# Sums over scan states and gathered rows by adding DMA transfers, a convolution as three products on TensorE, and new orders for the five queues

## The chip, the cores and the metric

The kernel runs on one core of one Trainium2 chip. A core has five engines that are programmed each with its own list of instructions: TensorE (PE) for matrix products, VectorE (DVE), ScalarE (ACT) and GpSimd (POOL) for element-wise work, and SyncE (SP), which here only issues DMA transfers. POOL also issues transfers, the indirect ones among them. Each engine takes its instructions strictly in the order of its list and waits at an instruction until what that needs is there. On chip there are two memories: SBUF (128 partitions), which all engines and the DMA engines reach, and PSUM, into which PE writes and from which DVE and ACT read. Everything else lies in DRAM.

The metric is the device time of one execution in microseconds, lower is better.

## The reference, cut to what matters

Eight sequences of 1024 tokens with 128 channels go through two layers. Each layer has two parts, and each part adds its result to `x`:

```python
x = x + L0_attn(layernorm(x))   # linear attention with a decaying state
x = x + L0_ffn(layernorm(x))    # 8 experts of width 352, two of them per token
x = x + L1_attn(layernorm(x))   # convolution over 3 tokens, then a selective scan
x = x + L1_ffn(layernorm(x))    # 8 experts of width 128, two per token, and 2 shared ones
```

The change touches `L1_attn` and the ends of the two expert parts. Of the third part:

```python
x = u @ Win + b_in
x = xp[:, :-2] * w[:, 0] + xp[:, 1:-1] * w[:, 1] + xp[:, 2:] * w[:, 2] + b   # xp: x with a zero token at both ends
x = silu(x)
dt = softplus(x @ Wdt + bdt); Bm = x @ Wb + bb; Cm = x @ Wc + bc
dA = exp(dt[..., None] * A)                                # 16 states per channel
dBx = dt[..., None] * Bm[:, :, None, :] * x[..., None]
h = dA_t * h + dBx_t                                       # token by token
y = einsum('bdn,bn->bd', h, C_t)                           # the sum over the 16 states
return y * silu(u @ Wg + bg) @ Wout + bout
```

In an expert part the result of a token is the sum over its two chosen experts, each weighted.

## The kernel before, in words

**Tiling.** A sequence's `x` stays in SBUF as 128 partitions by 1024 columns (8 chunks of 128 tokens). The attention parts work with channels in the partitions and the 1024 tokens along the columns, so that one DVE scan instruction runs over all tokens of one state.

**Order of the work.** The program writes every step as an operation with an engine, an estimated time, and the buffers that it reads and writes (`op`, and helpers such as `tt`, `stt`, `act`, `mm_cols`, `load`). The generators `l0_attn`, `l0_ffn`, `l1_attn` and `l1_ffn` of several sequences are advanced in turn by a table of times (`TIMES`); that gives the operations and their dependencies. In which order each engine then takes them is written out by hand in `ORDER`: one string per engine (PE, DVE, ACT, POOL, SP) that names for each place the sequence and how many of its waiting operations are skipped. `Schedule.run` walks through these five strings with the estimated times, gives each buffer a place in its group (four `st`, one `y`, four `tmp`, and so on), and emits the instructions. The estimates decide which of the free places a buffer gets, not the order itself. Several sequences are in work at once; the parts of different sequences are interleaved on each engine.

**The scan (`state`, L1251).** For each of 16 states ACT computes `da` = exp(dt * A), PE spreads B over the partitions into a PSUM tile `wide`, DVE multiplies it by `dtx` (in L561), DVE scans (L1262) into one of four `st` tiles, PE spreads C, and DVE multiplies `st` by it. The product of state 0 goes straight into the tile `y`; for each later state POOL adds `st` to `y` (L561, on POOL). There is a single `y` tile, so the scans of the sequences follow one another on it. Seven sequences work on all 1024 tokens at once; the last one takes its tokens in two halves, so its tiles have 512 columns.

**The head of `l1_attn`.** PE multiplies by `win` into PSUM (L610). ACT copies the result with its bias into a padded tile `xp`, ACT forms the first tap into `xs`, DVE adds the other two taps with two `scalar_tensor_tensor` (L567), and ACT applies silu.

**The expert parts.** `dispatch` normalises, routes, and scatters the token rows into a DRAM table `xd` ordered by expert, with 16 indirect transfers from POOL (L1029) that read `xw` and a copy of it in `tmp` (L1008). Blocks of 128 rows are then read back (`xg`), multiplied with the weights of their expert (`we` or `fe`, fetched by SP), weighted and written to a DRAM table `yd`. `combine` (L1041) gathers the rows of the first choice with 8 indirect transfers (L1048) into a `tmp` tile and adds the tile to `x` on POOL (L561), then does the same for the second choice. At most three such transfers are on their way at once (`ONWAY`).

**The first layer's scan.** `l0_attn` loads for each of 8 features a tile `kv` (512 KB, from `v_rows` in DRAM), multiplies it by `kT` (L561), scans it with `lam` (L935) and multiplies it by `qT` (L561), all on DVE, with all inputs in SBUF.

Of the kernel before, what the change touches and what calls it, by code (L numbers as in the profile page):

```python
# [11 lines left out]
F32 = mybir.dt.float32  # L12
# [6 lines left out]
P = 128  # L19
T = 1024  # L20
# [29 lines left out]

PE, DVE, ACT, POOL, SP = ENGINES = "PE", "DVE", "ACT", "POOL", "SP"
HOP = 0.1
TABLE = 1.3
ONWAY = 3


FREE = "wide", "acc", "row", "tile64", "xg", "xgT", "h", "ysb"
# [19 lines left out]
        0a0a0a0c0b0a0a1a1a1a1c0a1a0a1a0a0b0a0a0a1a0a1a1a1a2a1a1a2a2a2b2a2a0e0a1a0a0a0f0a0a0a1a0b0a2a  # L77
        0a0d0a0a0f0a1a0b0a0g0a0a0a0a2a0b0a0a0d0a2a0b0a0e0a3a0a0a3a0f0c3a3c0a0a0a0a3a0b3a0a0c0a0a0a0d
        0a2a0b0a0a0d0a2a0a3a0a0a0a2a1a3a0a1a1c1a1f1a1a1a3a1a1k1a1e3a1b1a1a1a3a1b1a1g3a1b1a1a1a1b1a1b
        1a1a1a1a1b1a1h1c1a1a1a1h1a1b1a0a1a0a0a2a1b2a0a0a1a2a1a1a0a1a0b1c0c0a0a1g1a0b1a0a1b1a0a0a1a1b  # L80
        0a0a1a1a0d0b0a0d1a0c0a0b2a0a2d0a2h2a2a0a2a2a2a0a0a2b2a0a2e2a0a2a2b2a0a0a2e2b2a2a0b0a2c2a2a2c
        0a2g0a2b2a0a2i2a2a2a2a0a0a2b2a2a1a2a2e1a2b1a0a2b2a0a1a1a2a0b0b2b0b0a0a2a2a0a1a2a1a0a1a2a2b2a
        2a1a2b1a2a1b2a2a1a3a2a3a1a2b2a2a2a3a1a0a1d0a1a0c0a0a1a0c0a1c2a0a1a1e0a0b0a1a0c1a0a1a0b1c0a1a
        0a4a0a1a4b0a4c0b0a0d4a0c0a1b0a1b4a1b1a4a0b0a1c1a1a0c1a0a0a1b0a0b1a0a3a3a3a0a0b0a1a0a3a3a3b3d
        3a3a2a3f3a3a3h3a2a3b3a2a3a3a3b3a4a1a3a2a2a3a4a1a3a3a3a4a3a3a3a3b3f3b3i2b3a2a2a3a3b5a3a5a5a5b
        3c5a3b5a1a3a1a3a1b1b3a3d3a3g3a1a3a2b1a3b3a1a3a1a2c3a3e2a1a3a2c3a4a3b2a3a3a2b2b2a3a2b2c3a4a4a
        1c1a2a1b1a2a1d2a1a4a2a1a2a1a2a1a1b2b1a2a2b1a1b1a2a4a2a1a1b2a1a5a1a1b4a2b1b1d1a2c2a1b1a2c1c1b
        2a1a2a1b1a2a1a1c1b1a5a1b1a3a1a3a3a4a4a4h4c4a4a4i4a4a5a4a4a5a4b3a4a4a4a3a2a4b4a4a2a4a4a4a4a4c
        4a4a3a4a3a5a4a2a3a4c4a2a3a2b2c4a4b2b2a4a2a4a5a2b4a3a4a2a4a4a3a4a3a4a3a4a4b4a3a4c4a3a4a5a3a4b
        4a4a3b5a3a4a2a4a2a4a4a3a4a2c3a5a4a2a3a4a2a4a2a3a2a2a3a3a3b2c4a4a3a2a2a2a3b2a3a2a2c3b2a3c3a2a  # L90
        3e2a2a3a2a6a3b2d2c6a3a2a6a2b3b3a2a6a2a6a2a6a2b3a2a3a2d2c2a2a6a2a2a2a5a5b5a5b5f5b5a6a4a5a4a4a
        5a3a6a3a4a3d4a5a3a3a5b3a3a5b5a3a3a4a5b5a4a5a4a5a4a5h5a5a4a4b4a5a5b5a5a5b5a7a5a4a7a4a5a5b5a7a
        5a3a7a3b3a3a3a7a5a5a7a5a3c5c3a5a3a5a3c5a4a5b5a5b3a5a5c3a5b5a3c5a5a4a5a5b5a6a5a4a5a3a5a3a5a7a
        5a5b5a3a3b5a3a6a4a6a4a3a3a3a3a4a3c3b7a4a3a4a6a3c3a4b4a6a3a4a3b4a3b3a6a3a4b3a4a4b7a3a3a4b4b4c
        4b3a4a5a4a5a4a5a3a5a4a6e6a5a7a6b6a6b6a5a6a5c6c7a5b6b6f6a7a6a6a6a4a4a6a5a6a6a6c6b6a5a6e6a6a5a
        4a6b6a4a4b6a6d6b6a4b4a5a6a4a6a6d4a6a5b6a5a6a4b5b6a6a4a6a6b6a5a6a5a6a7a6a5b6b6a5a6b6a7a6a5a6a
        4a6a4a6a7a4c6b6a5a6a5a5a4a5b6a4a4a5a6a4b4a5a5b6a5c4c6a5a4c4a5a4a5b4a5c4a4d4a4b5a5b5a4a5b5a4a
        4a4a4b7a7a7a4a7a7a7a4a7a7b7a4a5a7c4d7a4a7a7a4a5a4a7a4a7c4a4a7a4c7a7a7a7c4a7a4a6a7a7a4a7a7c7a
        6a7a6a7a7b7a7e7i7b7a5a7a7a7a6a6a7c7a5a7a5c5b7a7a7a5c5b5a7b7b7e7b6a7a5a5a7b7a7a6a7d7a7a6a6a7c
        7b6a7a6a7a6b6a6c6a6a5a5b5a5a6b5a5a5b6c6a6b5b5a6a6a5a5a5c6c6a5a6a5b5a6a5a5a6a5d6c5c6a5a6a5a5a  # L100
        5a7a5a6b5b6a5b5a7a6a5b5a7a5a5b7a6a5a6a7a6b5a5a6a5a5a7a7b7c7c7b7b7c7b7a6a6a7b7a7a6a7a6a7a6b6b
        6b6a7a7d6a7b7a7c7d7a6a7c7c7a7j7b7b7a6a7b7a7a7a7d7a7c7c6a7c6b6a6a7c7b7b6a6c6a7b7a7a6b7a6a7a6a
        7c7b7a6a7d6c7a7a6a6b7a6a7b7b6c7d6a7b7a6a6c7e6b7a7a7a6a7b7a7a6a7c7a6b6c7b7a6a7a7a6a7b6a7b6b6a
        6d6c6a7a6a6a6a6a7z7b7a7a7a7a7a7a7a7a7b7a7a7a7a7a7b7b7c7c7a7a7b7b7a7b7e7b7a7a7b7c7a7b7a7b7g7b
        7c7a7b7c7a7a7b7b7a7b7b7c7a7a7a7b7b7a7a
    """,
    DVE: """
        0a0e0a0a0a0a1a0a1e1a1bwawa0a0a0a0a0a0a0a0a1a1a0a1a0b0d0b0a0a0a0a0a0a0a0a0a0b0a0a0a1b1a1a1a0b
        1d0a1d1e0a0e0a0b0a0a1a1c0a2a1a1b1c1a0a0a2e0a0a0a0a0a0a0a0a0a0a0a0d0d0s0a0a0a0a0a0m0a0a0a0a0d
        1b0a0c2b0c0c0c0a1a2a2a2a1b1a1a1b1a2a1a1b1b0a1a1a1a1a1a1b1d1a1a1a3a1a3e3a3b3a2b2a2a0a3a2a0a2a  # L110
        2a0a2a1a1a2d2a1a2a0a1a1a1a2a1a1a1a0a1a1a1a1a1d1d1a1a1a1a1a0a1m1a1a1a1a1a3a1h1a1b1b1b1b1b2a0a
        2a0a2d2a0a2c2c2a0a1a2a2a0a2c0a2c2a0b0a0a0a2a2a3a3a0a3a0a3b3b0a3c3b3b0a3a3b0a3a2a3a0a3a3a3a3b
        0a3b3b3a2a1a3a1a3a3a1a3a3a3a1a1a1a3a1a3a1a1a1a1a1a0a2a2a2a2a2b2a1a0b0a0a0b0a2a0a1a1a1a0a0a0a
        0a2a2a1b1a2a2a2a2a2a2a2a2a2a2a2e2e2t2s2a2a2a0a2a2a2a0d2a2a2a2a2a2c2c2c0a2a0a0b2a0a0a0a0b2a2a
        1a0b0a0a0a0a1a0b0a0a1a0a0a0a1a1a0a0a0a0b0a0c0a0b0c0a0b0b0b0a0a0a2a2a0a0a2a0a0a0a2a0a2a0a0a2a
        0a0a0a2a2a0b0b0a2a0a0a0a0a2a1a2a1e1a1a1a1a0a2a1a0a0a0a0a0a0a0a3a0a2a4a2a3b3a3a3a0a3a1b1b3a1b
        4b4a2a4a4a0a0a1a0a0a0a0a2a0a0a0a0a0a0a0a0a0a0a0a1a0c1d0c0c4a0a1a0b1a0a0a0a0a0a0i0a0a0b0b0b0a
        0a0b0a0a0a1a1a2a2a0a1a1a0a1a1a1a2a1a2a1a1a4a2a1a1a1a2a3a3a1a3a3a3a3a3a3a3a3a3a3a3a3a3c3c3a3q
        3a3o3a3a2a3a3a3a3a3a3a3a3a3a3a3a3a1g0a1a1a1a0a1a1a1b1a0a1b1b0a1f1a1a1a1a1b1a0a1b1a1a0a0a1b1b
        1b1b0a1a4a1a0a1a1a1a1a1a0a1c1a4a1a0a1a2a2a2d0a3a2b2a1a2a3a4a2a4b4b4a3a2a4e3a4b4a3a4c2a4a4b3a  # L120
        4b3a4b1a2a2a3a4b1a4a3a4a4a4b4a4a2a1a2d2a4b2a3a2a2a4b5a3a5b1a5d5a5a5a1a1a1a3a3a5a2a2a2a1b1a2a
        2a1a4a3a4a5b5a5c5a3a3a1a1a5b1a1a1a1a1a1a1a5a1a1a1a1z1a1a1a1a1a1e1a1b1b1b3a1a1m1a1a1a1a3a1d1d
        2b1d1f1d1d2b1a1a1a5b3a1a5b1a2c2c3a5b1a3a2a2c2c5a2a3a3a2b2a2a2a4a4a4a2b2b4e4a4b4a4a1b2a1a4a2b
        2a2a2a2a2a2a1a2a2a2b1a2b2c2c1a2b4a4a2a2a4a4a4a4a4a2a4a4a4a4a4a1a4e4a4a4a4b4a4a4a4m4m4a4a4a4a
        4a4a4b4b4a4a4a4a2a1a2b2a2a2b1a2b2c5a5a1a2c5b2a2a1a3a3a3b3a3a5a3a5c3a1a5c1a5g2a5g5a5b4a3a5b4a
        3a5a5a4a3a5b5a3a4a4a2a4a2a3a4a4a2a2a3a3c3a3a4a2a2b2a2a3a4a2a2a3a3a5a3a3a3a4a2a4a2a3a2a2a2a2a
        2a2a2a2a2a2a2a2a2a2a2a2e2e2c2a2a2b2b2b2b2a2j2j2a2c2c2a2b2b2c2b4a2b2a5a5a5b4a2b3a3a2a5a5a5a3a
        4a4a3a3a5a3a3a5a4a3a6a4a3a3a3a4a4a3b6b6a6a6a5a5a3a6a5a5a5a5a5a5a5a5a5a5a5a5a5a5b5a5a5p5o5a2a
        5a4a3a3a3a5a4a5a5a5a5d5d5d5d5a5c5a3a5a3a2a3a3a4a2a3a3a3c3a3a3a6a3b2a3a2a3a3b3d3a3a3b2a2a3a3b
        3b3c3a3b3b3a2b2a6a3a6a6a6b3a6a2a3a6a6a6a2a6a2a6a6a6a4a4b4d4a4a4a3a5a4a6a5a3a3d3a3a3a6a6c6a3a  # L130
        5a4b6a6a6a4b4b5a4a3a3a3a3a3a3a3a3a3a3a3a3a3a3a3a3a3a3a3a3c3a3b4a3a3a3a3a4d4a4a3a3a3i4a3h4a3h
        3c3a3b3b3d3b3a5b3a7a3a7b7d7a7a5a3a4a7a4a7a4a4a5a4a4a5a4a4a4b4a4a5a5a5a4a5a4a5a3a6a6c6a7a5a3a
        6b7d7a7e3a7a5a7a5a4a5a3a6b7a5a4a5a6a7b4a5a7b4a7a5a7a7a5a3a7a7a7a5a4a7a7a3a6a4a7a6a4a6a6e6b3a
        4b6a6a6a7b6a4a4a4a4a3a4a7a3a4b4a6a6a4a6a6a4a6a6a6a6a6a4a6a6a6a6a6d6d6a6r6a6a6a6a6m3a6a6a6a6a
        6d6d6a6c6a6a6a6a4a4b4a4a7a4b5a4b3a4b5a5d5a5a5a4b5a4b4b4a4a4a4a5b7a4a5b5b3a7a7a7a4a4a5b5a5d5a
        5a5b6a5a6a6a5a5a7a5b5b4a6a7a6a4a4a6a5b4a4a6a4a4a4b4a7a5a4a7a5a6a7a5a6a7a5a4a4a6a7a4a4a4a4a4a
        4a4a4a4a4a4a4a4a4a4a4e4a4d6a4b4q4c4c4c4c4f4a4i4e4a6a4d4f4a4c4c5a6a4a4a5a4a5b5b6a5a4b7a7a5b6a
        4a5b6a5a6a6a5a5a5a6a5a7a7a6a5a7a7a7a7a7a7a7a7a7a7a7a7a7c7a7b7a7a7a7m4a7m7a6a7a7a7a7d7a7c7c7c
        7c5a5a5a6a5a7a7a5a5a4a5a6a5a5a5a4a5b5b5c5a5b5c4a5a4a5b5c5a5b5a4a5a4a5a5a5a7a4a7a7a5a7a4a5a7b
        7a5a4a4a6a5a6e5a7a5b5a5a7a6b6a6a5a6a6a6a5a7a4a7a7a7a6a7a6a6a7a7a6a6d5a5a6a6a7a6a6a5J5a5a5a5a  # L140
        5a7a5a5a5a5a5a5a7a5a5a5a5a5a5d5d5b5a5a5a5a5l5a5j5a5a5a5a5a5a5a5a5a5a7a6a5a6a5a7a6a7a6a7a6a6a
        6a7a6a6a6a6a6e6a6a6a6b6a5a5a6b6b6c6c6c6a6a5a6a5a6a6a6a6a6a5a6a5a6a6a7a7e7b7a7a7a6a7a6a5a6a6a
        5a6a6a7a6a5a7a6a7a7a5a6b6a6a7a6a5a7a5a7a6a6a7b6a7a7a7d7a7a7b7c7c7b7b7e7b7b6a7b6a6a6a6a6d6a6a
        6a7a6a7c7a7b7a7a7a7a6a6a7a6a6a6a6a6a6a6a6a6a6a6a6a6a6a6a6c6a6a6b6o6b6o6b6b6b6b6e6e6e6e6e6b7a
        6a6d7a7e7b7a6c7a7b6a7c7e7a7b7c6a7d6a7d7a7b7b7b7a7a7a7a7a7b6a7f7a7a7d7e7a7d7e7e7a7c7c6a6a7c7c
        7c7c7a7a7L7a7O7a7a7I7I7a7a7G7G6a7a7a7b6a7a7a7e7a7a7a7b7c7a7b7b6a7e7a6a7a7a7g7b7m7a7a7a7a7b7a
# [1342 lines left out]
```

## Time and profile before

| | |
|---|---|
| median of the runs (two) | 1825.53 us (1820.12 and 1830.94) |
| profiled execution | 1821.74 us |
| its span, first to last instruction | 1820.0 us |
| mean granted TensorE clock | 0.859 |
| ACT table loads | 171, 219.4 us |
| DMA | 283.59 MB, mean 156 GB/s |

| window, us | PE busy | DVE busy | ACT busy | POOL busy | DMA share |
|---|---|---|---|---|---|
| 0 to 120 | 63.7 | 79.0 | 39.6 | 3.6 | 0.94 |
| 120 to 300 | 153.8 | 120.1 | 73.6 | 68.7 | 0.71 |
| 300 to 600 | 226.5 | 242.2 | 193.6 | 161.6 | 0.51 |
| 600 to 900 | 235.8 | 261.4 | 183.2 | 160.4 | 0.55 |
| 900 to 1200 | 239.7 | 251.6 | 170.0 | 160.8 | 0.58 |
| 1200 to 1500 | 229.2 | 228.4 | 178.9 | 179.9 | 0.54 |
| 1500 to 1640 | 84.1 | 121.2 | 87.0 | 94.4 | 0.35 |
| 1640 to 1740 | 71.0 | 86.8 | 48.6 | 54.2 | 0.28 |
| 1740 to 1820 | 62.7 | 40.2 | 21.6 | 20.0 | 0.30 |

The profile is of one execution. A row of its groups names the line, the engine and the operation, then the tile written and the tiles read, the shape, and the number of instructions; behind the bar stand the busy microseconds of them all and the mean nanoseconds of one; behind the next bar the idle time of the engine just before them and what ended most of it. L561 and L610 are lines of helpers (`tt` and `mm_cols`), so there the tiles tell which step it is. The answers for one tile give the minimum, median and maximum of an instruction in place of the mean. The "chain" is the sequence of steps that ended last, followed back from the end; its shares say where the time to the end went. In the chain in order of time each piece has its start and its length in microseconds; a DMA piece runs from the issue to the landing. Of a DMA queue the page gives the packets, the megabytes and the share of the time of all 16 DMA engines that the packets took.

The scans of the second layer run on the tile `y` from 360 us (sequence 0) to 1733 us (sequence 7).

### The profile page before, as it was taken

How to read it: one execution, taken by the hardware profiler on the slowest of the kernel's cores; microseconds unless marked ns; L12 is line 12 of the kernel's file. 1: busy time of each engine (PE TensorE's matmuls, PEld its weight loads, DVE VectorE, ACT ScalarE, POOL GpSimd, SP SyncE). 2: the span in 40 equal slices, each digit the busy share in tenths (PEclk: the TensorE clock that was granted, in tenths of full speed). 3: DMA queues.
4: the chain of work that ended last, by engine and by line, in shares of the span. 5: the costliest groups of instructions: out<-in, count | busy, mean ns of one | idle time of the engine just before them, and what ended most of it. 6: DMA issues, size and time to landing. Idle time of an engine off the chain costs nothing.

```text
span 1820.0 us, 23716 instructions
## 1 busy us (share of the span) xinstructions
PE 1366.3 (75%) x7053; PEld 931.1 (51%) x7053; DVE 1430.9 (79%) x2188; ACT 996.2 (55%) x1707; POOL 903.6 (50%) x677
## 2 busy tenths in 40 slices
PE   4658898768777778768877878876887796646778
PEld 1115666446564546436664446633665765423545
DVE  4795683698896979996898886999889358888946
ACT  3325343856865575645755556356755476753632
POOL 0032504185368604876368632277457547667440
PEclk7868999789978999888988889868997998866699
DMA  8967786346455655554656447642565755312332
GB/s 185 224 150 187 216 258 196 98 139 190 139 150 165 206 150 148 140 168 154 180 148 199 130 123 232 194 120 79 175 176 172 217 174 154 105 58 63 103 103 64
DMA packets 215992, 283.59 MB, mean 156 GB/s; under 512 B 24376, under 2 KB 173368, under 8 KB 215864
## 3 DMA queue, kind: packets, MB, share of 16 engines
q1 hardware_dynamic: 200504, 250.46, 48.7%
q0 software_dynamic: 15360, 31.61, 5.7%
q8 instruction: 57, 0.93, 0.2%
q14 instruction: 71, 0.58, 0.1%
HBM read 224.73 MB, written 63.15 MB: 158 GB/s over the span
## 4 chain that ended last, share of the span: by engine, by line
DVE 44%; PE 26%; DMA 9%; ACT 9%; issue 8%; POOL 3%; another core or an unknown queue 1%; SPq 0%; DVEq 0%; ACTq 0%; POOLq 0%
DVE st L1262 10%; PE wide L610 7%; DVE wide L561 6%; PE wide L1141 5%; DVE kv L935 4%; DVE kv L561 4%; DVE st L561 4%; DMA kv<-v_rows 4%; PE wide L948 4%; DVE h L561 3%; PE acc L800 3%; DMA we<-w_rows 2%; DVE tile L561 2%; PE acc L1120 2%; DVE stats L629 2%
## 5 line engine op out<-in xcount | busy, mean ns | idle before, releaser
L1048 POOL DMA_INDIRECT tmp<-yd,at x240 | 265.3, 1106 | 197.1 <-DMA xg<-xd 82.8
L561 POOL TENSOR_TENSOR y<-y,st 128x1024 f32<-128x1024 f32 (+1 forms) x135 | 291.1, 2157 | 141.0 <-DVE st L561 116.7
L1141 PE MATMUL wide<-xgT,we 128*128 128x128 f32 x2208 | 303.0, 292 | 42.5 <-DMA we<-w_rows 14.2
L1141 PEld LDWEIGHTS wide<-xgT,we 128*128 128x128 f32 x2208 | 282.6, 205 | 73.3 <-issue 16.3
L1262 DVE TENSOR_TENSOR_SCAN st<-da,wide 128x1024 f32<-128x1024 f32 (+1 forms) x128 | 274.1, 2147 | 6.9 <-POOL y L561 2.0
L610 PE MATMUL wide<-term,eye3b 96*128 96x512 bf16 x512 | 190.3, 457 | 101.5 <-DVE st L1262 49.8
L1029 POOL DMA_INDIRECT xd<-xw,at x120 | 132.7, 1106 | 238.4 <-DVE at L786 191.8
L533 ACT ACT_TABLE_LOAD x171 | 219.4, 1283 | 3.8 <-PEq L1475 0.7
L1120 PE MATMUL acc<-we,h 128*128 128x128 f32 x1104 | 167.9, 292 | 42.1 <-DVE h L561 22.3
L1095 ACT ACTIVATE ysb<-acc,xg 128x128 f32<-128x128 f32 x345 | 116.6, 362 | 147.9 <-PE acc L1120 70.1
L1120 PEld LDWEIGHTS acc<-we,h 128*128 128x128 f32 x1104 | 149.2, 202 | 76.8 <-issue 27.8
L561 DVE TENSOR_TENSOR h<-h,wide 128x384 f32<-128x384 f32 x184 | 99.5, 545 | 106.2 <-ACT h L586 78.3
L586 ACT ACTIVATE h<-wide 128x384 f32<-128x384 f32 x184 | 89.4, 490 | 160.9 <-PE wide L1141 133.3
L561 DVE TENSOR_TENSOR wide<-dtx,wide 128x1024 f32<-128x1024 f32 (+1 forms) x144 | 158.2, 1102 | 19.2 <-PE wide L610 18.0
L586 ACT ACTIVATE da<-dt,a_mat 128x1024 f32<-128x1024 f32 (+1 forms) x144 | 149.0, 1050 | 34.8 <-DVE st L1262 28.5
L948 PE MATMUL wide<-kv,sum_e 128*32 128x512 f32 x256 | 139.8, 701 | 36.9 <-DVE kv L561 35.7
L561 DVE TENSOR_TENSOR st<-st,wide 128x1024 f32<-128x1024 f32 (+1 forms) x135 | 147.0, 1096 | 15.0 <-PE wide L610 6.9
L935 DVE TENSOR_TENSOR_SCAN kv<-lam,kv 128x1024 f32<-128x1024 f32 x64 | 150.6, 2358 | 0.7
L1029 POOL DMA_INDIRECT xd<-tmp,at x120 | 124.7, 1039 | 48.2 <-issue 35.6
L1008 POOL COPY tmp<-xw 128x1024 f32<-128x1024 f32 x15 | 16.7, 1112 | 228.8 <-ACT xw L645 172.7
L610 PEld LDWEIGHTS <-eye3b 96*128 96x128 bf16 x512 | 57.1, 112 | 141.2 <-issue 130.9
L1372 PE MATMUL acc<-xgT,fe 128*128 128x128 f32 x644 | 111.6, 329 | 11.1 <-ACT xgT L589 6.5
(155 smaller groups left out, 2293.5 us busy)
## 6 DMA issues: line engine op xcount, KB each, us to landing
we<-w_rows SPq DMA_DIRECT2D x184, 544.0 KB
fe<-f_rows SPq DMA_DIRECT2D x177, 192.0 KB
kv<-v_rows SPq DMA_DIRECT2D x64, 512.0 KB
xg<-xd SPq DMA_DIRECT2D x165, 129.0 KB
yd<-ysb SPq DMA_DIRECT2D x165, 128.0 KB
xd<-zrow SPq DMA_DIRECT2D x4, 1483.5 KB
x<-in_x_dram SPq DMA_DIRECT2D x8, 512.0 KB
v_rows<-tmp SPq DMA_DIRECT2D x8, 512.0 KB
```

Of the source, the lines that this page charges most:

```text
L533: nc.scalar.add_instruction(mybir.InstLoadActFuncSet(name=nc.get_next_instruction_name(), act_func_set_id=tables[table], ins=[], outs=[]))
L561: op(eng, us, lambda: e.tensor_tensor(out_(), in0(), in1(), alu), r, w)
L586: op(ACT, act_us(n), lambda: nc.scalar.activation(out_(), in_(), func, **kw), r, w, table)
L610: nc.tensor.matmul(dst.f[:m, c0 + s * HALF : c0 + (s + 1) * HALF], lhsT(), rhs()[:, ts(s, HALF)], start=True, stop=True,)
L935: lambda kv=kv: nc.vector.tensor_tensor_scan(kv.f, lam.f, kv.f, 0.0, ALU.mult, ALU.add),
L948: nc.tensor.matmul(py.f[rows, ts(s, HALF)], sum_e[:, j, :], kv.f[:, ts(s, HALF)], start=(j == 0), stop=(j == FGRP - 1),)
L1029: lambda k=k, c=c: nc.gpsimd.indirect_dma_start(out=views[k * NC + c], out_offset=bass.IndirectOffsetOnAxis(ap=v3(at, TOPK, NC)[:, k, c : ...
L1048: lambda k=k, c=c, g=g: nc.gpsimd.indirect_dma_start(out=v3(g, NC, P)[:, c, :], out_offset=None, in_=yd[i], in_offset=bass.IndirectOffsetO ...
L1095: lambda: nc.scalar.activation(v3(ysb, 2, P)[:, i % 2, :], py.f[:, c0 : c0 + P], AF.Copy, scale=v3(xg, 2, XW)[:, i % 2, P : P + 1],),
L1120: nc.tensor.matmul(py.f[:, :P], v3(h, 3, P)[:, j, :], we.f[:, c0 : c0 + P], start=(j == 0), stop=(j == 2),)
L1141: nc.tensor.matmul(p4[:, m, j, :], we.f[:, c0 : c0 + P], xgT.f[:, ts(i % 2, P)], start=True, stop=True,)
L1262: lambda: nc.vector.tensor_tensor_scan(f(st)(), f(da)(), f(pb)(), last.f[:, n : n + 1] if t0 else 0.0, ALU.mult, ALU.add),
```

## The change

There are four parts.

1. In `state`, the add of `st` to `y` is no longer a POOL instruction but a DMA transfer issued by POOL that reads `st` from SBUF and adds it to `y` in SBUF (`accum_op`). This holds for the seven sequences with 1024 columns (105 transfers of 512 KB); the last sequence keeps its 30 adds on POOL.
2. In `combine`, the 16 gathers write into no tile of their own: each adds its rows to its chunk of `x` (`compute_op`). The two POOL adds and the two `tmp` tiles fall away.
3. In `l1_attn`, the three taps of the convolution are folded into three copies of `win` (`win3`, computed once), and PE sums three products with shifted columns in PSUM. The biases are folded into three columns (`conv_bias`: inner tokens, first token, last token). ACT applies silu from PSUM, and once more for each of the two end columns. `win` and the spread taps are loaded into a `tmp` tile at the start.
4. All five strings of `ORDER` are new. The estimates behind the run through them have changed too: many times, an overlap between neighbouring operations of an engine (`OVERLAP`), and a mark for operations that hold the port that DVE and POOL share into SBUF (`HOLDS`: DVE operations with all inputs in SBUF, POOL's element-wise work) or that start only when it is free (`AWAITS`: POOL's transfers). These estimates choose among free places and don't add instructions. `TIMES` is as it was. The new ACT order has 185 table loads. The tile of zeros that fills `xd` is now a `tmp` tile, and SP's order at the start is another: among others, a zero fill of `xd` and the last part's shared weights stand ahead of the first store of `v_rows`.

The core of the diff (the five order strings and the changed estimates are left out):

```diff
...
+HOLDS, AWAITS = 1, 2
+OVERLAP = {PE: 0.15, DVE: 0.08, ACT: 0.1, POOL: 0.0, SP: 0.0}
-HOP = 0.1
+HOP = 0.05
...
-                start = max(clock[e], o.ready)
+                start = max(clock[e], o.ready, way if o.port else 0.0)
...
+    def make_taps():
+        nc.vector.tensor_tensor(
+            win3, win.f[:, :P].unsqueeze(1).to_broadcast([P, 3, P]),
+            win.f[:, P : 4 * P].rearrange("p (c k) -> p k c", k=3), ALU.mult,
+        )
...
+    op(DVE, 1.4, make_taps, [loaded["in"], win], [tapped])
...
     def combine(x, i, at):
...
-            g = Buf("tmp")
             for c in range(NC):
                 line(
-                    lambda k=k, c=c, g=g: nc.gpsimd.indirect_dma_start(
-                        out=v3(g, NC, P)[:, c, :],
+                    lambda k=k, c=c: nc.gpsimd.indirect_dma_start(
+                        out=x3(x)[:, c, :],
...
+                        compute_op=ALU.add,
                     ),
-                    [yd_b[i], at], [(g, c)], 2.5,
+                    [yd_b[i], at, (x, c)], [(x, c)], 2.4,
                 )
-            tt(lambda: x3(x), lambda: x3(x), lambda g=g: v3(g, NC, P), ALU.add, T, [x, g], [x], POOL)
...
     def l1_attn(x, b):
...
-        mm_cols(p0, P, lambda: win, lambda: uT.f, [uT, *ssm])
...
+        def taps():
+            for s in range(T // HALF):
+                lo, hi = s * HALF, (s + 1) * HALF
+                for j, k in enumerate((1, 0, 2)):
+                    a0, a1 = max(lo, 1 - k), min(hi, T + 1 - k)
+                    nc.tensor.matmul(
+                        p0.f[:, a0:a1], win3[:, k, :], uT.f[:, a0 + k - 1 : a1 + k - 1],
+                        start=(j == 0), stop=(j == 2),
+                    )
+
+        op(PE, 6.2, taps, [uT, tapped, *ssm], [p0])
...
-        op(DVE, 0.2, edges, [p0], [xp])
-        act(lambda: xp.f[:, 1 : T + 1], lambda: p0.f, AF.Identity, T, [p0, xp], [xp], bias=b_in)
         xsf = lambda: xs.f
-        act(xsf, lambda: xp.f[:, 0:T], AF.Identity, T, [xp], [xs], scale=convw[:, 0:1], bias=convb)
-        for k in (1, 2):
-            stt(
-                xsf, lambda k=k: xp.f[:, k : k + T], convw[:, k : k + 1], xsf, ALU.mult, ALU.add,
-                T, [xp, xs], [xs],
-            )
-        act(xsf, xsf, AF.Silu, T, [xs], [xs], "silu")
+        act(xsf, lambda: p0.f, AF.Silu, T, [p0, tapped], [xs], "silu", bias=conv_bias[:, 0:1])
...
     def state(n, t, dt, dtx, bc3, y, last):
...
-        if n:
+        if n and w == T:
+            op(
+                POOL, 1.26,
+                lambda: nc.gpsimd.dma_start(f(y)(), f(hc)(), accum_op=ALU.add),
+                [y, hc], [y], land=4.0, port=AWAITS,
+            )
+        elif n:
             tt(f(y), f(y), f(hc), ALU.add, w, [y, hc], [y], POOL)
...
```

## The prediction

> **What bounds the kernel now.** First the page's busy shares, then its chain that ended last:
>
> ```profile
> PE 1366.3 (75%) x7053; PEld 931.1 (51%) x7053; DVE 1430.9 (79%) x2188; ACT 996.2 (55%) x1707; POOL 903.6 (50%) x677
> DVE 44%; PE 26%; DMA 9%; ACT 9%; issue 8%; POOL 3%; another core or an unknown queue 1%; SPq 0%; DVEq 0%; ACTq 0%; POOLq 0%
> ```
>
> DVE is the busiest engine and holds 44% of the chain: 801 of its 1431 busy us lie there. PE holds 26% (473 of 1366 us). In the windows of 300 us from 300 to 1200 DVE is busy 242, 261 and 252 us. So a microsecond taken from DVE is worth between 801/1431 = 0.56 us (the chain's share) and 1820/1431 = 1.27 us (if DVE keeps its duty of 78.6%).
>
> Next the groups with shapes kept apart, and the minimum, median and maximum of the same instructions in the answers for the tiles kv and tile:
>
> ```profile
> L561 DVE TENSOR_TENSOR wide<-dtx,wide 128x1024 f32<-128x1024 f32 x112 | 136.6, 1221 | 16.0 <-PE wide L610 15.0 <-remote 0.7
> L561 DVE TENSOR_TENSOR kv<-qT,kv 128x1024 f32<-128x1024 f32 x64 | 85.4, 1340 | 0.5
> L561 DVE TENSOR_TENSOR tile<-tile,row 128x64 f32<-128x64 f32 x45 | 23.4, 519 | 1.3
> L567 DVE SCALAR_TENSOR_TENSOR xs<-tmp,convw,xs 128x1024 f32<-128x1024 f32 x16 | 24.0, 1500 | 17.1 <-ACT xs L586 16.9
> ```
> ```profile
> L561 DVE TENSOR_TENSOR kv<-qT,kv x64: 1194/1218/3833, 37.2 to 1258.6; 128x1024 f32<-128x1024 f32 x64
> ```
> ```profile
> L561 DVE TENSOR_TENSOR tile<-tile,row x51: 184/224/6130, 109.6 to 1797.5; 128x64 f32<-128x64 f32 x45, 128x32 f32<-128x32 f32 x6
> ```
>
> The same product costs 1221 ns on average when one input is in PSUM and 1340 when both are in SBUF, though their medians are alike (1222 and 1218); a 224 ns operation once took 6130. The long ones stand beside POOL's adds:
>
> ```profile
> L561 POOL TENSOR_TENSOR y<-y,st 128x1024 f32<-128x1024 f32 x105 | 253.1, 2410 | 110.5 <-DVE st L561 101.4 <-DVE row L583 2.9 <-DVE row L561 2.4
> L561 POOL TENSOR_TENSOR x<-x,tmp 128x1024 f32<-128x1024 f32 x30 | 72.3, 2410 | 23.1 <-DMA tmp<-yd,at 22.6
> L1048 POOL DMA_INDIRECT tmp<-yd,at x240 | 265.3, 1106 | 197.1 <-DMA xg<-xd 82.8 <-issue 56.8 <-DMA yd<-ysb 21.1
> ```
>
> So POOL is half idle itself, but its adds stretch DVE. Last, the queues, and three pieces of the chain:
>
> ```profile
> q1 hardware_dynamic: 200504, 250.46, 48.7%
> q0 software_dynamic: 15360, 31.61, 5.7%
> ```
> ```profile
> 810.09 4.34 DMA kv<-v_rows
> ...
> 1260.72 2.37 POOL y L561
> 1263.26 2.26 DMA tmp<-yd,at
> ```
>
> A 512 KB load takes 4.34 us from issue to its user, a 64 KB gather 2.26, a POOL add 2.37. q1 moves 250.46 MB in 48.7% of 16 x 1820 us, so 17.7 KB per us and engine: 512 KB (32.8 KB an engine) spend 1.85 us on the way.
>
> **The change part by part.** All sums are against the profiled execution: span 1820.0, own time 1821.7; the median of the runs shown is 1825.5, 3.8 higher.
>
> *POOL adds leave, DVE gets its port back.* Of 363 us of POOL adds (291.1 of y, 72.3 of x), 325 go; the last sequence's 30 half-size adds (38 us) stay. What DVE pays for them is count x (mean - median) of its rows with two SBUF inputs: kv products 64 x 0.116 + 64 x 0.122 = 15.2; kv scans 64 x 0.074 = 4.7; tile,row 45 x 0.295 = 13.3; tile,rank 4.4; gbias 3.2; pair 1.9; row on row 6.2 + 4.2; row<-stats 3.7; dt, dtx and bout 6.2. Sum 63 us; 90% of it, 57 us, goes.
>
> *Convolution.* 16 scalar_tensor_tensor on xs go from DVE (24.0 us) and 16 memsets (1 us); the tap weights cost DVE some 2 us once (three products like the 1218 ns rows at a third of the size, six one-column operations), in the start-up, where DVE is busy 79 of 120 us. DVE: -57 - 24 - 1 + 2 = **-80 us**. PE runs three products where it ran one: win takes 18.6 us in all, so +37 us. ACT loses two passes of 8 (8.9 + 9.9), gains 16 one-column activations (3 us at the 183 ns of the one-column copies), and its new order has 185 table loads for 171, 14 x 1.28 = 18: together about nothing. The head of the scan stays as long (4.7 us more of PE for 1.11 + 1.24 + 2.6 less of ACT and DVE) but crosses engines less often: 17.1 us of DVE idle before xs and 11.7 us of ACT idle behind it are at stake. I take 10.
>
> *The accumulating transfers.* No row shows one. POOL's issue is near the gather's 1106 ns, so 105 issues are 116 us for 253, and the 240 gathers stay. From issue to landed: the gather's 2.26 plus 7/8 of 1.85 for eight times the bytes is 3.9, the plain load 4.3. If the destination is read in a pass of its own, 1.85 more: 5.7 to 6.2. Bounds 4 and 6, none below, since as many bytes must move; I take 5, the middle. Each waits for the one before it on y, and POOL stands behind that wait with the gathers and scatters queued after it; their user DVE meets it through xg, and through the four st places, which now stay taken until the landing. The question is whether 15 links fit into the DVE work between a sequence's first and last state product. In the changed kernel's DVE order that work, at the medians (scan 2.28, product 1.22, h 0.55 ...), is 73, 76, 105, 89, 111, 88 and 62 us for sequences 0 to 6; at a duty of 0.8 (0.865 for the last, as in 1500 to 1640) 91, 95, 132, 111, 138, 110 and 71 us. Against 15c: c = 5 asks 75 and stretches only the last, by 4 us; c = 6 costs 19; c = 8 costs 29 + 25 + 9 + 10 + 49 = about 121.
>
> Here a rule speaks against the change. The Trainium skill (SBUF — State Buffer, section "SBUF: two separate sides") warns of transfers issued from POOL: while DVE holds the shared port pair, POOL can't write the descriptors, and it advises issue from SP or ACT. By the rule an issue may stand for a whole 2.28 us scan, 105 x 2.28 = 239 us of POOL. The row says less: gathers take 955 ns at the median, 1106 on average, 0.15 us each, 16 us for 105. POOL would carry either (about 694 us of work left); on a chain link it is 0.15 against 2.3, so c = 5 or above 7. I take the row.
>
> *DMA.* 105 x 512 KB are 55 MB more, 11% of 16 engines' span on top of 55%. DMA holds 9% of the chain, some 100 us of it behind the start; waits longer by a tenth are +10, and the weight and kv loads share the engines. I take +12.
>
> *Gathers into x.* Two adds of 2.4 us at the end of a combine go, and one or two of the four tmp places are free that held gathered rows; POOL's waits do not set the end (3%), so I count nothing. Without that cover it would be a gain.
>
> *Order.* All five lines are new. SP's start puts a zero fill and the last layer's weights ahead of v_rows: up to 8 us late, up to as much early elsewhere. I take 0 with 36 us to each side.
>
> Sum: DVE -80 x 1.27 = -102 (the duty, not the chain's share, since the new order is written around the freed time; -45 by the share), PE +37 x 473/1366 = +13, chain links +4, DMA +12, scan's head -10: **-83**. Span 1737, own time 1739, **1741 us** by the runs' median.
>
> **Rivals.**
> *The gain stays off the end* (0.20): PE, then with 1403 us of work the busiest, takes over; DVE's time counts 0.56: -45 + 37 (PE at full) + 4 + 12 - 10 = -2, to -40 with PE at its share: 1785 to 1823. For it: PE is busy 236 and 240 us of the 300 from 600 to 1200. Against: PE holds only 26% of the chain.
> *Slower* (0.13): an accumulating transfer costs far more than a move, because source and destination are read and DVE and other loads interrupt it. From c = 7.5 us the chain on y eats all of the 83 us; at 8.5 it costs 159, hence 1901. For it: dense stages, sequence 6 with 62 us of DVE work for 15 links. Against: 64 KB gathers land in 2.26 us.
> *The change doesn't free DVE* (0.07): the issues of POOL hold the port as the adds did. Then -24 x 1.27 + 13 + 4 + 12 - 10: about 1814. Against: laid beside POOL's timeline, some 64 us of the excess of DVE's long operations overlap its adds and 2 us its DMA issues.
>
> **How the numbers follow.** The forecast has 0.60, with its own range 1690 to 1790 (DVE between 0.56 and 1.27, c between 4 and 6, the order's 36). Below 1690 I leave a tenth of that. The slower case and the first rival draw the upper end: 1680 to 1850 leaves out some 0.15. Under 2%, about what a measurement of this kernel can tell from no change, is 1789 to 1862. Faster 0.72 (forecast, and half of the first rival), same 0.17, slower 0.11.
>
> **What would show it.** The kv products' mean falls from 1340 to about 1235 and tile,row from 519 to 250; DVE's busy time to 1350; PE's to 1403; POOL's to about 690. Landing of the y transfers shows as DMA waits of POOL and of DVE's scans on st: if these sum to over 80 us, the slower rival holds. Wrong I would be if c is above 7, or if the new order's idle time outweighs what DVE no longer does.

## The result and the profile after

The changed kernel takes 1881.95 us (median of two runs, 1878.17 and 1885.73) where the kernel before takes 1825.53: a ratio of 1.031, interval 1.026 to 1.036. It is slower, by some 56 us. The prediction was 1741 us, with a range of 1680 to 1850. The profiled execution is the one of 1885.73 us, its span 1883.9 us.

The page of the changed kernel: busy shares and the two DMA queues that carry the transfers.

```profile
PE 1417.9 (75%) x7117; PEld 963.9 (51%) x7117; DVE 1352.8 (72%) x2163; ACT 999.1 (53%) x1721; POOL 806.6 (43%) x647
...
q1 hardware_dynamic: 200648, 250.66, 46.5%
q0 software_dynamic: 57360, 86.67, 25.5%
```

DVE lost the 78 us of work that it was to lose (80 predicted). But its idle time, span less busy, grew from 389 to 531 us, so its share fell from 79 to 72%. The queue of POOL's transfers went from 5.7% to 25.5% of the DMA engines' time.

The groups with shapes kept apart; behind the bar the busy microseconds and the mean of one in ns, then the idle time before them:

```profile
L1081 POOL DMA_INDIRECT x<-yd,at x240 | 400.8, 1670 | 257.9 <-DMA yd<-ysb 108.4 <-issue 66.7 <-DMA xg<-xd 50.1
...
L1317 POOL DMA_DIRECT2D y<-st x105 | 108.7, 1035 | 322.4 <-DVE st L567 155.6 <-DMA y<-st 120.4 <-issue 16.0
...
L567 DVE TENSOR_TENSOR kv<-qT,kv 128x1024 f32<-128x1024 f32 x64 | 77.4, 1217 | 0.4
...
L1211 PE MATMUL wide<-xnT,win 128*128 128x512 f32 x64 | 31.2, 610 | 0.5 <-ACT xnT L596 0.4
...
L1211 PE MATMUL wide<-xnT,win 128*128 128x511 f32 x32 | 16.5, 597 | 0.0
...
L567 DVE TENSOR_TENSOR tile<-tile,row 128x64 f32<-128x64 f32 x45 | 12.5, 278 | 1.2
```

The product on `kv` fell from 1340 to 1217 ns and `tile,row` from 519 to 278: POOL's adds no longer stretch DVE. The issue of an adding transfer takes POOL 1035 ns. The gather that adds takes it 1670 ns in place of 1106, and its rows travel as 512 B packets.

The waits, before (first fence) and after (second), as the list of waits gives them (microseconds in all, times, longest):

```profile
ACT h L586 <- PE wide L1141: 133.3, 86, 6.6
...
DVE h L561 <- ACT h L586: 98.6, 62, 6.5
...
PE wide L1141 <- DMA we<-w_rows: 14.2, 15, 2.9
...
PE acc L1072 <- DMA xg<-xd: 5.9, 6, 2.1
```
```profile
DVE h L567 <- ACT h L593: 195.0, 96, 9.9
...
ACT h L593 <- PE wide L1174: 138.8, 88, 6.4
...
POOL y L1317 <- DMA y<-st: 120.4, 32, 8.0
...
DVE st L1302 <- DMA y<-st: 15.3, 14, 3.7
...
DVE y L567 <- DMA y<-st: 14.8, 4, 8.2
...
PE acc L1105 <- DMA xg<-xd: 10.3, 6, 6.4
```

Two things are new. POOL waits 120 us for the landing of the addition before, DVE's scans 15 us for an `st` that a transfer still reads, and DVE another 15 us for the last landing on `y`; before, none of these could be. And DVE now stands 195 us for ACT at `h`, the product inside an expert block, 96 us more (with the waits at `h` that the list books to other causes, 212 for 137, so 75 us more). ACT's own wait for PE at `h` in the first layer's blocks hardly grew (133 to 139). The change leaves the operations inside an expert block as they were; only their place in the order is new.

PE's busy time grew by 52 us, more than the 29 us that the further products of the convolution take (18.6 us before, 31.2 and 16.5 in the two rows above). The rest lies in products that the change leaves alone; the mean granted clock was 0.859 before and 0.840 here.

In windows of 300 us from 300 to 1200 DVE is now busy 205, 228 and 219 us (242, 261 and 252 before), and the DMA share is 0.66, 0.78 and 0.77 (0.51, 0.55 and 0.58).

### The profile page after: what moved, and what is told of

Same layout as the page of the kernel before. It is cut to its first block, busy times and chain, and to the rows that moved or that the text cites. A ratio compares the mean times of both kernels' runs of the same rounds, so it can differ in the third digit from the quotient of the medians.

```text
span 1883.9 us, 23492 instructions
## 1 busy us (share of the span) xinstructions
PE 1417.9 (75%) x7117; PEld 963.9 (51%) x7117; DVE 1352.8 (72%) x2163; ACT 999.1 (53%) x1721; POOL 806.6 (43%) x647
## 3 DMA queue, kind: packets, MB, share of 16 engines
q0 software_dynamic: 57360, 86.67, 25.5%
## 5 line engine op out<-in xcount | busy, mean ns | idle before, releaser
L1081 POOL DMA_INDIRECT x<-yd,at x240 | 400.8, 1670 | 257.9 <-DMA yd<-ysb 108.4
L1174 PE MATMUL wide<-xgT,we 128*128 128x128 f32 x2208 | 308.6, 296 | 27.3 <-ACT xgT L596 11.5
L1174 PEld LDWEIGHTS wide<-xgT,we 128*128 128x128 f32 x2208 | 289.9, 210 | 56.6 <-ACT xgT L596 18.3
L1317 POOL DMA_DIRECT2D y<-st x105 | 108.7, 1035 | 322.4 <-DVE st L567 155.6
L1153 PE MATMUL acc<-we,h 128*128 128x128 f32 x1104 | 178.0, 304 | 67.8 <-DVE h L567 45.8
L1153 PEld LDWEIGHTS acc<-we,h 128*128 128x128 f32 x1104 | 155.8, 211 | 107.6 <-DVE h L567 45.9
L1418 PE MATMUL acc<-xgT,fe 128*128 128x128 f32 x644 | 125.9, 358 | 32.3 <-DMA fe<-f_rows 13.9
L982 PE MATMUL wide<-kv,sum_e 128*32 128x512 f32 x256 | 127.6, 657 | 24.5 <-DVE kv L567 22.9
L1418 PEld LDWEIGHTS acc<-xgT,fe 128*128 128x128 f32 x644 | 113.8, 262 | 55.1 <-ACT xgT L596 23.1
L596 ACT COPY xgT<-acc 128x256 f32<-128x256 f32 (+1 forms) x180 | 64.5, 360 | 145.3 <-PE acc L1105 128.9
```

Source lines behind the costliest of these rows:

```text
L982: nc.tensor.matmul(py.f[rows, ts(s, HALF)], sum_e[:, j, :], kv.f[:, ts(s, HALF)], start=(j == 0), stop=(j == FGRP - 1),)
L1081: lambda k=k, c=c: nc.gpsimd.indirect_dma_start(out=x3(x)[:, c, :], out_offset=None, in_=yd[i], in_offset=bass.IndirectOffsetOnAxis(ap=v3( ...
L1153: nc.tensor.matmul(py.f[:, :P], v3(h, 3, P)[:, j, :], we.f[:, c0 : c0 + P], start=(j == 0), stop=(j == 2),)
L1174: nc.tensor.matmul(p4[:, m, j, :], we.f[:, c0 : c0 + P], xgT.f[:, ts(i % 2, P)], start=True, stop=True,)
L1418: nc.tensor.matmul(p13.f[:, ts(n * m + q, P)], w[q].f[:, ts(m, P)], xgT.f[:, ts(q, P)], start=True, stop=True,)
```

## The experiments

Four theories. **S**: the y transfers lost the time, either by their load on the DMA engines (**L**) or by the chain of their landings (**K**). **G**: the gathers that add lost it. **C**: the convolution did. **O**: the new orders did, whatever stands in them. A ratio is always to the kernel before, run beside it on the same chip, and 1% of it is 18 us. The runs come from three chips, with the kernel before between 1800 and 1842 us in the median, so only ratios are compared; from their intervals the difference of two is good to some 0.6 to 0.8%.

### Taking parts back in the new order

The first kernel puts the y sums back on POOL:

```diff
-    lambda: nc.gpsimd.dma_start(f(y)(), f(hc)(), accum_op=ALU.add),
+    lambda: nc.gpsimd.tensor_tensor(f(y)(), f(y)(), f(hc)(), ALU.add),
```

> The changed kernel with the y sums as POOL instructions again, all else kept. Theory S: the 55 MB and the chain of landings leave, 1810 to 1840. Theory G: the loss stays and the port contention comes back, 1890 to 1950. Theory O: 1880 to 1940.

Measured: 1.053 (1.049 to 1.057). Slower still than the changed kernel, so in its own order the y transfers are a gain, of about 2%. Theory S in its plain form falls; and since neither the chain nor the load of the y transfers is left here, something else takes more than 5%.

```profile
PE 1397.7 (74%) x7117; PEld 952.5 (50%) x7117; DVE 1413.6 (75%) x2163; ACT 998.9 (53%) x1721; POOL 978.2 (52%) x647
```
```profile
DVE h L567 <- ACT h L593: 201.4, 98, 9.9
...
ACT xgT L596 <- PE acc L1105: 162.2, 83, 9.1
```

The long wait of DVE at `h` is there without a single adding y transfer (the page's busy line, then two lines of its waits).

Three more kernels took back the gathers, both sums, or all three parts. The gathers need `tmp` tiles that the new order has given to others, so steps had to trade places:

```diff
-    for e, o in heads.items():
+    for o in [*(o for e in rest for o in rest[e][:far]), *drift]:   # far: 1, or 2, 3, ... in a circle
```

> The changed kernel with gathers that write into a tmp tile and two POOL adds for each expert part, all else kept. Theory G (each gather costs POOL 1.67 us instead of 1.11 and its rows go in 512 B packets): 1780 to 1820, POOL's issue time of the gathers down from 401 to about 265 us. Theory S: 1875 to 1895. Theory O: 1870 to 1900.

> The changed kernel with both adds on POOL again; convolution on PE and the new orders are kept. Theory G and theory S: 1800 to 1830 (the convolution's gain or loss beside 1825). Theory O: 1880 or more.

> The five orders and the estimates of the changed kernel, with the three other parts undone: y sums and gathered rows added by POOL instructions again (gathers into tmp tiles), convolution with one product and two taps on DVE. Steps that the new order doesn't know are put in when they are ready, and where the strict order would stand in a circle the nearest later step goes first. Theory O (the new order itself lost the time): 1880 us or more. Theory G (the gathers that add into x) or theory S (the transfers that add y): 1825 give or take 25, as the kernel before.

Measured: 1.120, 1.131 and 1.160. With the order disturbed like this, they tell nothing about the parts. In the third the gathers stand 159 us behind DVE's `dt`, a wait that is not in the changed kernel. They show only that the new order can't carry the old steps. The old order can carry the new ones, so the rest was done from there.

### One part at a time in the old order

In the kernels with the gathers or the convolution, steps that the old order doesn't know are put in when they are ready, and where the engines would stand in a circle the nearest later step goes first. The rest of the order is as before.

The y transfers in the old order, seven sequences as in the change:

```diff
+    if w == T:
+        op(POOL, ..., lambda: nc.gpsimd.dma_start(f(y)(), f(hc)(), accum_op=ALU.add), [y, hc], [y])
+    else:
         tt(f(y), f(y), f(hc), ALU.add, w, [y, hc], [y], POOL)
```

> The kernel before with one part of the change: the 105 y sums as transfers that add, orders and all else as before. The prediction's sum for this part (DVE's port freed of 291 of 363 us of adds, about 50 us of DVE; 12 us more of DMA, 4 of chain): 20 to 50 us faster than before, a ratio of 0.97 to 0.99. Theory S (these transfers lost the time): a ratio above 1.01, with DMA waits of POOL and of DVE's scans on st above 80 us.

Measured: 1.043 (1.037 to 1.050), 79 us slower. Here theory S holds, though DVE is relieved as planned (busy 1391 us, 40 less). POOL waits 168 us for landings, and DVE itself 73:

```profile
DVE y L561 <- DMA y<-st: 42.6, 3, 14.9
...
DVE st L1262 <- DMA y<-st: 30.7, 15, 4.6
```

The gathers:

```diff
-    out=v3(g, NC, P)[:, c, :],
+    out=x3(x)[:, c, :], compute_op=ALU.add,
-    tt(lambda: x3(x), lambda: x3(x), lambda g=g: v3(g, NC, P), ALU.add, T, [x, g], [x], POOL)
```

> The kernel before with one part of the change: the 240 gathers add into x and the 30 POOL adds go, orders and all else as before. Theory G (the gather that adds costs POOL half a microsecond more and eight times the packets): a ratio of 1.02 or more. Prediction (no cost): 0.98 to 1.00. If the gathers stand so early in the old order that they must now wait for x, that shows as a wait of POOL for other engines' work on x and is a cost of the order, not of the gather.

Measured: 1.001 (0.999 to 1.004). Theory G falls for the gathers alone. POOL works 71 us more, the rows take 9.8% of the DMA engines in place of 5.7%, and nothing of it reaches the end.

The convolution (the three products and the silu from PSUM as in the change, the removed steps' places left empty):

> The kernel before with one part of the change: three products for the convolution, no taps on DVE, silu from PSUM; orders as before, the taps' weights and the zero tile put in at the start when they are ready. Prediction for this part: DVE -24 us, PE +37 to 52, the head of the scan shorter by 10 in all: a ratio of 0.98 to 1.00. Theory C (the convolution's PE time lost it): a ratio above 1.01.

Measured: 1.005 (1.003 to 1.008). A small loss where a gain of 26 us was in the sum. DVE's busy time fell by 23 us, but its wait for ACT at `h` rose from 99 to 144 us: the freed time turned into waiting.

```profile
DVE h L564 <- ACT h L589: 143.9, 65, 9.9
```

All three:

> The kernel before with all three parts of the change and the old orders. Theory O (the new orders lost the time): a ratio of 0.95 to 0.98, well below the changed kernel's 1.03. Theories G, S and C (a part lost it): a ratio near 1.03 or above.

Measured: 1.052 (1.047 to 1.058). The parts alone make the kernel slower than the changed one is. So the new order helps these parts, by 2.0%, and theory O in its plain form falls too. The waits of this run show what the new order is good for:

```profile
DVE h L564 <- ACT h L589: 154.9, 83, 10.9
...
DVE y L564 <- DMA y<-st: 57.9, 4, 20.9
...
DVE st L1314 <- DMA y<-st: 54.7, 17, 8.3
```

DVE waits 113 us for landings here and 30 in the changed kernel, but 155 us at `h` here and 195 there. With the same three parts the new order spares DVE 82 us at the landings and costs it 40 at `h`; DVE's idle time is 579 us here and 531 there. Convolution and gathers without the y transfers:

> The old order with the convolution on PE and the gathers that add, y summed on POOL: the same parts as in the changed kernel with its y sums back on POOL, which was at 1.053. If the parts' times add, 1.00 to 1.01; then the difference to 1.053 is what the new order costs by itself. If convolution and gathers cost only together, 1.03 or more.

Measured: 1.019 (1.015 to 1.023), more than the sum of the two. POOL, with the slower gathers and all the adds, is at 53% there and holds 10% of the chain that ended last (3% before):

```profile
DVE 37%; PE 23%; POOL 10%; DMA 10%; ACT 9%; issue 9%; SPq 1%; DVEq 0%; POOLq 0%; ACTq 0%
```

This run carries the same parts as the changed kernel with its y sums back on POOL, which was at 1.053. The difference, 3.3%, is what the new order costs as long as POOL sums y. DVE works the same in both, 1408 and 1414 us; its idle time is 427 us in the old order and 474 in the new. The waits of the run in the old order:

```profile
DVE h L564 <- ACT h L589: 149.2, 69, 9.9
...
ACT xgT L592 <- PE acc L1102: 93.4, 65, 5.9
...
PE wide L1171 <- DMA we<-w_rows: 17.7, 18, 2.7
```

In the new order with the same parts these are 201.4, 162.2 and 2.3. The new order waits less for weights, and more from engine to engine.

### The bytes, the chain and the issue

The same 105 transfers with an eighth of the bytes:

```diff
-    nc.gpsimd.dma_start(f(y)(), f(hc)(), accum_op=ALU.add)
+    nc.gpsimd.dma_start(y.f[:, :P], hc.f[:, :P], accum_op=ALU.add)
```

> The 105 transfers in the old order, but each adds only 128 of the 1024 columns; seven eighths of the sum are left out. Chain, issue and waits stay, the landing is shorter by the time that the bytes take, and the load is an eighth. Theory K with a link of landing plus 0.9 us: links of about 4 us instead of 6.5, so the scan stages shrink to near those of before and the freed port counts: a ratio of 0.98 to 1.00. If POOL's place in the queue and not the landing holds the chain: above 1.02.

Measured: 0.980 (0.976 to 0.984). Issue, waits and links are all there, and the kernel is 37 us faster than before: DVE works 41 us less, and its share stays at 79%. The bytes then cost 0.980 to 1.043, 6.3%.

Bytes do two things: they load the engines and lengthen each landing (from the start of the issue to the end of the last packet 3.3 us on average here, 5.6 with all the bytes). To part them, load without a chain:

```diff
     nc.gpsimd.tensor_tensor(f(y)(), f(y)(), f(hc)(), ALU.add)
+    nc.gpsimd.dma_start(spare[n % 8], some)      # 896 KB, DRAM to DRAM; 64 KB in the control
```

> The kernel before, y still summed on POOL, with a transfer of 896 KB from DRAM to DRAM issued by POOL behind each of the 105 adds; nothing waits for what it brings. It puts about the load of the adding transfers on the DMA engines without their chain. Theory L (the load slows the other transfers): a ratio of 1.03 or more. Theory K (the chain of landings on y is what costs): 1.00 to 1.01.

> The load run with 64 KB instead of 896 KB behind each POOL add: the same 105 further issues on POOL, nearly none of the load. Theory L: 1.00 to 1.01, so the 1.045 of the load run was load. If POOL's issuing was it: 1.03 or more.

Measured: 1.045 (1.040 to 1.051) with 896 KB and 1.020 (1.015 to 1.025) with 64 KB. The issues behind the adds cost 2.0% themselves, more than theory L allowed them; the load costs 2.5%. The same load behind the small transfers:

> The old order, y transfers of 128 columns (seven eighths of the sum left out) and behind each of them a transfer of 832 KB from DRAM to DRAM that nothing waits for: the chain of the small transfers with the load of the whole ones. If the load is the smaller part of the 6.3% between 0.980 and 1.043 and the chain the larger: 1.00 to 1.015. If the load is nearly all: 1.035 or more.

Measured: 1.033 (1.026 to 1.041), from 0.980: 5.3%, of which the 105 further issues are a part. That is just under what the expectation set for "nearly all". The small transfers (first two fences) and the same with load (last two), busy time and waits:

```profile
PE 1338.2 (76%) x7053; PEld 912.9 (52%) x7053; DVE 1389.9 (79%) x2188; ACT 996.2 (57%) x1707; POOL 753.7 (43%) x677
```
```profile
DVE h L561 <- ACT h L586: 124.6, 72, 7.2
...
PE wide L1141 <- DMA we<-w_rows: 15.9, 19, 2.0
...
PE acc L1072 <- DMA xg<-xd: 15.5, 11, 3.1
```
```profile
PE 1391.3 (74%) x7053; PEld 953.5 (51%) x7053; DVE 1388.0 (74%) x2188; ACT 998.4 (53%) x1707; POOL 818.7 (43%) x782
```
```profile
DVE h L563 <- ACT h L588: 161.4, 90, 10.1
...
PE acc L1074 <- DMA xg<-xd: 48.9, 22, 7.1
...
PE wide L1143 <- DMA we<-w_rows: 35.5, 28, 3.3
```

DVE's work is the same. PE waits longer for the rows (`xg`) and the weights (`we`) of the expert blocks, and DVE, whose order is fixed, stands longer at the block's `h` behind ACT. PE's busy time grows too, by 53 us with the same 7053 products, at a mean granted clock of 0.847 for 0.874. By PE's share of the chain in the kernel before (473 of 1366 us) that would be some 18 us of the end, an estimate; whether the waits bring the lower clock or the lower clock the waits, no run here tells. The weights land 4.53 us after their issue on average, 4.17 with the small transfers, 3.97 before. So in the old order the load is worth between 2.5% (beside the adds) and 5.3% (issues included), and 1.0 to 3.8% is left for the longer chain. The traces add that DVE's own waits for landings are 73 us with whole transfers, 24 with small ones and 27 with small ones and the load. The runs don't part these further.

Smaller doses, transfers for every second or third state only:

> The old order with transfers for the seven even states of each sequence and POOL adds for the eight odd ones. Theory K: two links take 6.5 and about 2.7 us, 4.6 on average, less than the 5.3 us that a state takes in the densest stage before: 0.99 to 1.01. Theory L: half the load, half the loss: about 1.02.

> The old order with transfers for states 3, 6, 9, 12 and 15 of each sequence, POOL adds for the other ten. Between nothing (1.000), every other (1.004) and all (1.043): a curve with a gain that comes first and a cost that grows faster gives 0.995 to 1.003; below 0.99 it would beat both kernels.

Measured: 1.004 (1.001 to 1.007) and 1.006 (1.003 to 1.010). No dose tried is faster than the kernel before. Half the transfers meet theory K's number and not L's 1.02: they cost far less than half of what all of them cost. A POOL add between two transfers may break the chain, or the cost of the load may grow faster than the load; this is open.

### The small transfers in the new order

> The changed kernel with y transfers that add only 128 of the 1024 columns; seven eighths of the sum are left out. Theory L (bytes): 0.97 to 1.00 against before, 40 to 60 us below the changed kernel. Theory O (the new order is slow whatever the transfers bring): 1.02 to 1.03.

Measured: 1.010 (1.006 to 1.015), again with 128 of the 1024 columns. The bytes cost 2.0% here, a third of what they cost in the old order, and neither theory's number is met: without the bytes the new order is still slower than before. Its waits:

```profile
POOL y L1317 <- DVE st L567: 208.0, 26, 38.7
...
DVE h L567 <- ACT h L593: 193.7, 96, 9.9
```

DVE waits for landings only 1 us here, and still its idle time is 514 us, 125 more than before. The wait at `h` stays where it was at 195 us, so it isn't made by the y transfers' bytes. The gathers without their addition:

```diff
-                        compute_op=ALU.add,
```

> The changed kernel with gathers that overwrite their chunk of x instead of adding to it: the experts' second rows replace x, so the sums are left out; order and waits are the same. Packets are 4 KB again and POOL's issue 1.1 us. If the gathers' small packets carry a part of the loss: 1.00 to 1.02. If not: within 1% of the changed kernel's 1.03.

> Both of these together (seven eighths of the y sums and the sums over the gathered rows are left out): what the new order takes when neither transfer loads the DMA engines. Theory L: 0.95 to 0.98. Theory O: still above 1.01.

Measured: 1.027 (1.023 to 1.032), whose interval overlaps the changed kernel's, and 1.014 (1.007 to 1.022), no better than the small transfers alone. POOL is busy 140 us less and nobody gains by it.

## Why the prediction was wrong

Two ways lead in measured steps from the kernel before to the changed one:

| step | ratio after it | step alone |
|---|---|---|
| convolution and gathers, old order | 1.019 | +1.9% |
| the new order, y summed on POOL | 1.053 | +3.3% |
| y sums from POOL to transfers of an eighth | 1.010 | -4.0% |
| whole transfers | 1.031 | +2.0% |

| step | ratio after it | step alone |
|---|---|---|
| convolution and gathers, old order | 1.019 | +1.9% |
| y sums from POOL to whole transfers, old order | 1.052 | +3.3% |
| the new order | 1.031 | -2.0% |

The new order costs 3.3% with POOL's sums and saves 2.0% with the transfers; the transfers cost 3.3% in the old order and save 2.1% in the new one. Neither has a price of its own, so the loss can't be put on one of the four parts. In both ways the convolution and the gathers come first, in the old order, and lose 1.9% there, where the prediction had a gain; their price in the new order was not measured.

By the prediction's own steps:

- **DVE's work, -80 us.** Right: -78 in the profile, and the means of `kv` and `tile,row` fell to 1217 and 278 ns.
- **Its worth, 1.27 us for each, since DVE keeps its duty of 78.6%.** This is the step that failed most. The prediction took the duty as kept because the order was "written around the freed time". DVE's duty fell to 71.8%: 142 us more idle against 78 less work. In the new order the bytes are the smaller part of it. With an eighth of them in the same order DVE is idle 125 us more than before, and the kernel still takes 1.010, where the prediction without its 16 us for chain and DMA would be at 0.945; of the 141 us between forecast and result that is about 119. More than half of the 142 us, 75, stand at `h`. The wait for ACT there is 194 to 203 us in all five kernels in the new order left undisturbed and 99 to 168 in the twelve in the old one, the kernel before among them: it goes with the order. In the old order with small transfers the duty was kept (79%), and there 41 us of work gave 37.
- **The new order, 0 with 36 us to each side.** Taken as one number, it had none: +61 us with POOL's sums, outside the bound, and about -39 with the transfers, at its edge. It spares DVE waits for landings and adds waits at `h`. The prediction did name the case, "if the new order's idle time outweighs what DVE no longer does", and it is the one that came. Which entries of the order put DVE at `h` too early was not tried, so this cause stays open.
- **DMA, +12 us.** Mis-sized. It took waits for DMA as a tenth longer, on the 9% of the chain that they hold. In the old order the load costs 2.5 to 5.3%, 46 to 97 us; besides PE's waits for loads, DVE's waits for ACT and PE's busy time grow there. In the new order load and chain together cost 2.0%, 37 us, where the prediction had 16.
- **The chain, c = 5 us and +4.** The landing lay within the bounds of 4 to 6: 5.7 us on average in the changed kernel, 5.3 in the median. But a link is longer than its landing: where POOL waits for nothing else, the next issue mostly starts 0.8 to 0.9 us after it, and the 45 such links are 6.2 us on average. By the prediction's own list of stages c = 6.2 asks 24 us, not 4. And the scan stages were taken at a DVE duty of 0.8. Before, DVE is busy 96, 86, 91 and 86% of the time in the first four scan stages, so that there is less slack. In the old order the scan stage of sequence 0 goes from 79 to 110 us and that of sequence 3 from 122 to 148.
- **The issue of a transfer.** The trace's row was the right one to take against the rule that the prediction quotes: 1035 ns on average, 1560 at most, and no issue that stood for a whole 2.28 us scan. The rule was also stretched: the Trainium skill (SBUF — State Buffer, section "SBUF: two separate sides") gives it for DVE operations in a 2-port mode, and nothing here shows the scan to be one.
- **Gathers, 0.** Alone 0.1% in the old order, and no difference in the new one that these runs resolve. That POOL's issue grew from 1106 to 1670 ns was missed; together with the convolution and POOL's adds it may be what makes 1.9% of two parts that cost 0.1 and 0.5% alone, for POOL then holds 10% of the chain.
- **Convolution.** PE's products grew by 29 us (37 predicted), DVE lost its taps, but the 26 us of gain became a loss of 10.
- **PE's clock, no term.** PE's busy time grew by 52 us, 23 of them beyond the convolution, at the lower granted clock. What that is worth was not tried.

Two of the prediction's sums are off: by its own terms PE at its share gives -26 in the first rival, not -40, and 1901 us in the second counts the +4 of the chain twice. Neither changes the forecast.

The rivals: "slower" had the right sign, and its sign in the profile came (136 us of waits for landings of POOL and of DVE's scans, over its limit of 80), but at a landing of 5.7 us and not its 7.5 to 8.5. It would put the loss on the y transfers, and in the changed kernel they are a net gain over POOL's sums. "The gain stays off the end" has a part of the truth: the freed time turned into waits of DVE, though not for PE's capacity, which is at 75% as before. "The change doesn't free DVE" is out.

## What to carry to other kernels

A saving on the busiest engine counts only with the order that it runs in, so before it is multiplied by span over busy time, compare how the engine's idle time would change; a new order needs its own term and its own bound. A new order and the work that it was written for can't be priced apart: run each with and without the other. Moving work to the DMA engines is paid by everything that waits for a load, and in a kernel with fixed orders a part of that bill arrives as waits between engines, not as waits for DMA. For a chain of dependent transfers count landing plus wake-up, and take the slack from the stage where the chain runs, not from the mean.

## What the runs showed of the hardware

- A 4 KB packet that adds from SBUF to SBUF took 336 ns in the median; a plain one of the gathers before, from DRAM to SBUF, 192. No run here has a plain one from SBUF to SBUF. The 512 KB transfer lands after 5.3 us in the median, the 64 KB one (128 packets of 512 B) after 2.8 to 3.1.
- An indirect gather that adds moved its 64 KB in 128 packets of 512 B, about 66 ns each on average; without the addition in 16 of 4 KB, about 234 ns each. The time from the start of the issue to the landing rose from 3.0 to 4.1 us on average in the old order (4.5 in the changed kernel), and POOL's issue by half a microsecond.
- A transfer that nothing waits for still costs when POOL must issue it: 105 of 64 KB behind POOL's adds made the kernel 36 us slower, and DVE's busy time rose from 1431 to 1455 us. Laid over POOL's timeline, 87 of the 90 us by which DVE's operations exceed their medians there fall on operations that overlap POOL's adds (62 of 65 us in the kernel before), and 2 on those beside its DMA issues; why the adds then met DVE more often is open.
